# Cross-attention stages: ScalarE and VectorE in written order, norms in two pieces, the routing's norm behind a batch's second exponential

## The chip, the cores and the metric

One Trainium2 chip, of which one core is used. The time is the device time of one launch in microseconds (us), as the median of several runs. The engines are named as in the profile: PE (TensorE), DVE (VectorE), ACT (ScalarE), POOL (GpSimd) and SP (SyncE, which only issues transfers here). Each engine works through its own instruction stream in order and waits on semaphores for the others.

## The reference

Four layers act on `x` of shape (4, 512, 256) with a context `ctx` of shape (4, 64, 256). Each layer is an attention over the context, then a feed-forward part, both added to `x`.

```python
# layers 0 and 3: softmax attention, 16 heads of 16
q = _layernorm(x) @ Wq + bq;  k, v = ctx @ Wkv + bkv
x = x + softmax(q k^T / 4) v @ Wo + bo
# layer 1: the same over feature maps [exp(z), exp(-z)], z = heads @ fm_w^T + fm_b,
#          values of 32 per head, output through fc_w
# layer 2: a cosine alignment between x and ctx
# layers 0 and 3, feed-forward: 8 experts, 2 picked per token by a router
#          that works on _layernorm(x)
# layer 1: MLA self-attention, then a shared expert and 7 routed ones
# layer 2: a gated feed-forward with blockwise fp4 quantization
```

What matters here is a layer norm of every token, the projection to queries, scores against 64 keys per head, a largest score per head, an exponential, a sum and its reciprocal, the weighted values and the output projection; and in layers 0 and 3 a second layer norm of the result, router logits, the two best of eight experts and a table of where each token's row goes.

## The kernel before, in words

`x` stays in SBUF as 16 tiles of 128 tokens by 256 (`NT` = 16). Four tiles make one batch of the input (`GT` = 4, `B` = 4). The attention over the context of layers 0, 1 and 3 is one method, `xattn` (L637), called by `xattn_linear` for layers 0 and 3 and directly from `run` for layer 1. Below, L0, L1, L2 and L3 with no further number mean these layers; L followed by two or more digits is a line of the kernel.

**One batch's work** is divided into generators. `ctx_heads` (L618) is the front: layer norm of four tiles (`layernorm`, L326: per tile a `bn_stats` and a `bn_aggr` on DVE, one square root `ln_sd` on ACT, reciprocal `ln_rs` and shift `ln_sh` on DVE, then four Identity activations that write `xn`), the output bias added to `x` on POOL (L628), eight transposes (`ps_xT`) with copies to SBUF (`xnT`, in turn by ACT and DVE), the query projection (`ps_q`) and the batch's values (`ps_v`, `v`, `va`). `ctx_largest` (twice per batch, L516) computes scores `ps_cs` and their negative maxima `mx` (DVE); `ctx_turned` transposes these (`ps_mT`, `mT`). `ctx_weights` (twice per batch, L549) computes scores turned round in `ps_cx`, subtracts the maxima by four more products, and takes one exponential of 128 x 2048 (`cpr`, ACT, L563). There is a single PSUM buffer for `ps_cs` and `ps_cx` (`sc=1`, L642), so the next product there waits until its reader is done. `ctx_sums` sums the weights (`ps_den`) and takes the reciprocal `crs` (DVE, 128 x 512). `ctx_values` spreads `crs` over the head's columns (`ps_bc`, copied by ACT to `cbs`), multiplies with the weighted values (`ps_cy`, `cy` on DVE), and projects (`ps_p`, added to `x` on DVE).

**The routing** of a batch (`route`, L1143, in layers 0 and 3) has its own layer norm, eight transposes, router logits (`ps_r`, `r_lg`), the two best experts (`top2`, a chain of small DVE instructions), ranks by two small products (`ps_rank`), row addresses `e_at` (DVE), and eight indirect transfers of POOL that write the token rows to `xs` in DRAM (L859). From the second batch on a table of blocks is computed (DVE). SP then loads each expert block's tokens (`e_x`, L1008), which PE transposes (`ps_xe`, L1016) ahead of the block's large products (`ps_gu`). `begin` issues the first of these loads inside the last batch of `xattn`.

**The order.** A planner places instructions unless a region is entered with `in_order`, in which the engines named keep the order in which the Python code writes them. In `xattn` PE is in written order for the whole stage. In L1, where `before` is given, ACT, DVE and POOL are in written order too, for the first batch. The loop over batches interleaves three generators by hand with `some(gen, n)`, which advances a generator by n steps: `new`, the front of the next batch; `old`, `ctx_values` of the batch before, followed by its routing; and `late`, the rest of an older `old`. The list `soon` says how many steps of `new` go to each of five places. Behind a stage the expert blocks run in a region with DVE and SP in written order.

**Before L1** the results of L0's routed blocks are loaded from DRAM and added to `x` (`before.load`, `before.take`), on DVE for the first batch and on POOL for the others. L3 follows L2's feed-forward, whose fp4 steps (`f_y`, `f_c`, `f_am`) are on DVE and whose last product is `ps_fd` (L1655); L3's key copy `kT` (ACT, L427) and `kbd` (DVE, L399) come from the keys' product `ps_k`.

Of the kernel before, what the change touches and what calls it, by code (L numbers as in the profile page):

```python
# [14 lines left out]
PE, SP, ACT = mybir.EngineType.PE, mybir.EngineType.SP, mybir.EngineType.Activation  # L15
DVE, POOL = mybir.EngineType.DVE, mybir.EngineType.Pool
# [7 lines left out]
B, S, E = 4, 512, 256  # L24
# [3 lines left out]
GT = S // P  # L28
# [160 lines left out]
class Net:  # L189
# [425 lines left out]
                nc.vector.tensor_tensor(x, po[:, i], x, ALU.add)  # L615
            yield

    def ctx_heads(self, pool, st, query, values, bias, before):  # L618

        g = st.g  # L620
        if before:
            for i in range(GT):
                before.take(g * GT + i, self.nc.gpsimd if g else self.nc.vector)
        xn = self.xn_tile()
        self.layernorm(g, xn)
        for i in range(GT):
            x = self.x[g * GT + i]
            self.nc.gpsimd.tensor_tensor(x, x, self.row(bias), ALU.add)  # L628
        yield
        xT = self.transposed(xn)  # L630
        yield
        st.qs = query(pool, xT)
        yield
        st.va = values(pool, g)
        yield

    def xattn(self, query, values, scale, dv, W, bias, before=None, after=None, keys=None, begin=lambda: None):  # L637

        with self.room("xattn") as pool, self.banks(mm=4, sc=1), ExitStack() as stack:  # L642
            mxs = [pool.tile([P, 4, 32], F32, tag=f"mx{i}", name=f"mx{i}", bufs=1) for i in range(GT)]
            for m in mxs:
                self.nc.gpsimd.memset(m, 0.0)
            for t in range(NT if before else 0):
                before.load(pool, t, self.nc.scalar if t // GT == 1 else self.nc.sync, bufs=12)
            stack.enter_context(self.in_order(PE))
            if keys:
                for _ in self.ctx_ready(pool, keys):  # L650
                    pass
            sts = [SimpleNamespace(g=g, pr=[]) for g in range(B)]

            def heads(g):
                return self.ctx_heads(pool, sts[g], query, values, bias, before)

            def rest(st):
                yield from self.ctx_values(pool, st, dv, W)
                if after and st.g < B - 1:
                    yield from after(st.g)  # L660

            def some(gen, n=-1):
                while n and next(gen, self) is not self:
                    n -= 1

            nf = NH * dv // P
            old = late = iter(())
            new = heads(0)  # L670
            first = ExitStack()
            first.enter_context(self.in_order(ACT, DVE, POOL) if before else nullcontext())
            some(new)
            for st in sts:
                if st.g:
                    old = rest(sts[st.g - 1])
                new = heads(st.g + 1) if st.g + 1 < B else iter(())

                soon = [1, 0, 1, 1, 0] if st.g else [0, 0, 0, 1, 1]
                some(new, soon[0])  # L680
                self.ctx_largest(st, 0, mxs)
                some(old, 2)
                self.ctx_largest(st, 1, mxs)
                some(old, nf // 2)
                some(new, soon[1])
                self.ctx_turned(pool, st, mxs)
                some(new, soon[2])
                some(old, nf - nf // 2)
                some(late)
                if st.g == B - 1:  # L690
                    begin()
                self.ctx_weights(pool, st, 0, scale)
                some(new, soon[3])
                self.ctx_weights(pool, st, 1, scale)
                some(new, soon[4])
                some(old, 2)
                self.ctx_sums(pool, st)
                some(new)
                some(old, 2)
                late = old  # L700
                first.close()
            old = rest(sts[-1])
            for _ in old:
                some(late, 1)
            some(late)

# [90 lines left out]
class Routed:  # L799
# [282 lines left out]
    def begin(self, pool):  # L1082

        self.held, self.xb, self.wgu, self.wd = pool, {}, {}, {}

        self.weights(0, (True, False))
        for b in range(3):
            self.tokens(b)
        for b in range(1, 3):
            self.weights(b, (True, False))  # L1090
            self.tokens(b + 2)
# [41 lines left out]
    def take(self, t, eng):  # L1133

        x, r = self.net.x[t], self.loaded.pop(t)
        for k in range(2):
            eng.tensor_tensor(x, x, r[:, k], ALU.add)


class Layers(Net):  # L1140


    def route(self, moe, g, rw, fine=False):  # L1143


        def steps():
            rows = self.xn_rows()
            xn = rows[:, :, :E]
            yield from self.layernorm_steps(g, xn)
            moe.mark(g, rows)  # L1150
            yield True
            xT = self.transposed(xn)
            yield True
            lg = self.sm("r_lg", [P, GT, 8])
            self.nc.vector.tensor_copy(lg, self.scores(xT, rw, 8))
            yield True
            picked = self.top2(lg, 8, NEG, True, rows)
            yield True
            yield from moe.add(g, rows, *picked)
            yield True  # L1160

        return (whole for whole in steps() if whole or fine)
# [617 lines left out]
```

## Time and profile before

| | us |
|---|---|
| median of 3 runs | 1987.32 (1986.11 to 1991.52) |
| the profiled execution's own time | 1997.21 |
| its span | 1995.5 |
| PE busy | 1712.2 (86%) |
| DVE busy | 1020.4 (51%) |
| ACT busy | 671.4 (34%) |
| POOL busy | 424.3 (21%) |
| mean granted PE clock | 0.928 |

The three attention stages lie at about 0 to 165 us (L0), 535 to 704 us (L1) and 1560 to 1717 us (L3) of the span. PE is busy 119.1 of the first 165 us, 135.5 of the 169 us of L1's stage, and 123.7 of the 157 us of L3's.

In the profile, a line of the timeline gives start, duration, engine, line of code, operation, output and inputs, how many instructions it stands for, and in brackets the idle time of the engine just ahead of it with what ended that wait. A line of the waits gives what waited, for what, the total, how often and the longest. PEld is PE's loading of weights, which overlaps with its products.

### The profile page before, as it was taken

What the parts mean: (1) busy time and instruction counts of PE and PEld (TensorE: products, weight loads), DVE (VectorE), ACT (ScalarE), POOL (GpSimd) and SP (SyncE); (2) the same over time, 40 slices, a digit from 0 to 9 for tenths busy, and PEclk for the clock granted to TensorE, in tenths of its full rate; (3) what the DMA queues carried; (4) which work ended last, traced back from release to release, by engine and by line L of the source; (5) the groups of instructions that cost most, each with busy time, mean ns of one, the idle gap of its engine ahead of it and who ended that gap; (6) DMA issues with size and microseconds to landing.
All of it is one profiled execution on the core that took longest, in us unless ns stands there. A gap on an engine that the chain in (4) does not pass through costs nothing.

```text
span 1995.5 us, 25928 instructions
## 1 busy us (share of the span) xinstructions
PE 1712.2 (86%) x8752; PEld 970.5 (49%) x8752; DVE 1020.4 (51%) x3011; ACT 671.4 (34%) x1254; POOL 424.3 (21%) x594
## 2 busy tenths in 40 slices
PE   5878999999789868898989888985998887899993
PEld 2435666666444433343433344543665443455552
DVE  3655544444454343444454536546989565553333
ACT  3333222222254323335343432233445334222220
POOL 2031211111240021123131312223113103221112
PEclk8989999999899968998999999995899898999997
DMA  9528787887400100000001035972000001788884
GB/s 294 160 84 330 273 294 281 290 287 281 134 1 1 39 1 1 1 1 22 1 27 42 19 101 173 298 254 85 1 1 1 12 1 65 238 293 301 298 298 162
DMA packets 109350, 271.61 MB, mean 136 GB/s; under 512 B 13409, under 2 KB 71201, under 8 KB 99105
## 3 DMA queue, kind: packets, MB, share of 16 engines
q1 hardware_dynamic: 82976, 227.97, 33.9%
q0 software_dynamic: 10176, 28.00, 3.7%
q10 hardware_dynamic: 16064, 13.98, 2.1%
q8 instruction: 70, 1.15, 0.2%
q14 instruction: 64, 0.52, 0.1%
HBM read 220.48 MB, written 49.42 MB: 135 GB/s over the span
## 4 chain that ended last, share of the span: by engine, by line
PE 69%; DVE 18%; ACT 6%; issue 3%; DMA 2%; POOL 1%; SPq 0%; ACTq 0%; DVEq 0%; POOLq 0%
PE ps_gu L1030 20%; PE ps_de L1072 10%; PE ps_ms L1235 4%; PE ps_mo L1273 3%; DVE mq L1240 2%; PE ps_p L612 2%; PE ps_mx L1250 2%; PE ps_f L1633 2%; PE ps_xT L377 2%; PE ps_he L1059 2%; PE ps_bc L591 2%; ACT cpr L563 2%; PE ps_cx L557 1%; PE ps_ms L1238 1%; PE ps_cy L597 1%
## 5 line engine op out<-in xcount | busy, mean ns | idle before, releaser
L1030 PE MATMUL ps_gu<-e_wgu,e_xT 128*128 128x352 f32 (+1 forms) x1088 | 420.9, 526 | 13.1 <-DVE e_xT L1022 5.8
L1030 PEld LDWEIGHTS ps_gu<-e_wgu,e_xT 128*128 128x128 f32 x1088 | 195.5, 190 | 155.7 <-issue 71.4
L1072 PE MATMUL ps_de<-e_wd,e_hT 128*128 128x256 f32 x932 | 233.0, 387 | 10.8 <-ACT e_hT L303 3.1
L1075 POOL DMA_INDIRECT ys<-e_y,e_to x116 | 113.2, 976 | 482.6 <-ACT e_y L1074 336.5
L1072 PEld LDWEIGHTS ps_de<-e_wd,e_hT 128*128 128x128 f32 x932 | 172.8, 191 | 83.6 <-issue 39.0
L1047 DVE TENSOR_TENSOR e_h<-e_s,ps_gu 128x352 f32<-128x352 f32 (+2 forms) x155 | 83.4, 538 | 244.8 <-PE ps_gu L1030 185.0
L1240 DVE TENSOR_REDUCE mq<-ps_ms 128x2 f32<-128x256 f32 (+3 forms) x128 | 105.7, 826 | 139.9 <-PE ps_ms L1238 136.6
L1046 ACT ACTIVATE e_s<-ps_gu 128x352 f32<-128x352 f32 (+2 forms) x155 | 74.1, 478 | 280.3 <-PE ps_gu L1030 264.9
L1074 ACT ACTIVATE e_y<-ps_de,e_wt 128x256 f32<-128x256 f32 x116 | 55.0, 474 | 262.6 <-PE ps_de L1072 250.0
L1252 ACT ACTIVATE mpr<-ps_mx 128x1024 f32<-128x1024 f32 (+3 forms) x128 | 90.1, 704 | 146.9 <-PE ps_mx L1250 137.9
L1235 PE MATMUL ps_ms<-mkT,mqT 32*128 32x512 f32 (+3 forms) x512 | 111.7, 515 | 25.8 <-DVE mq L1240 24.3
L859 POOL DMA_INDIRECT xs<-xn,e_at x96 | 94.5, 985 | 120.4 <-DVE e_fi L893 39.7
L1250 PE MATMUL ps_mx<-mqm,mkT 32*128 32x128 f32 (+3 forms) x512 | 107.4, 497 | 1.3 <-ACT mpr L1252 1.3
L1254 POOL TENSOR_SCALAR_AFFINE_SELECT mpr<-mpr 128x256 f32<-128x256 f32 x128 | 52.2, 409 | 250.7 <-ACT mpr L1252 250.6
L1273 PE MATMUL ps_mo<-mpr,va 128*32 128x128 f32 (+3 forms) x512 | 97.1, 461 | 4.5 <-POOL mpr L1254 3.2
L1633 PE MATMUL ps_f<-w,xqT 128*128 128x352 f32 x256 | 86.1, 478 | 1.2 <-ACT xqT L1624 1.2
L1059 PE MATMUL ps_he<-consts_sb,e_h 128*128 128x128 f32 x466 | 76.3, 277 | 9.6 <-DVE e_h L1047 6.7
L557 PE MATMUL ps_cx<-q,kbd 32*128 32x512 f32 x256 | 45.2, 806 | 44.1 <-ACT cpr L563 44.1
L1235 PEld LDWEIGHTS ps_ms<-mkT,mqT 32*128 32x128 f32 x512 | 40.9, 195 | 80.6 <-DVE mq L1240 56.0
L1019 DVE COPY e_xT<-ps_xe 128x256 f32<-128x256 f32 x78 | 33.0, 423 | 86.7 <-PE ps_xe L1016 86.7
L377 PE MATMUL ps_xT<-consts_sb,xn 128*128 128x128 f32 x256 | 48.8, 330 | 32.4 <-ACT xn L345 18.7
L1059 PEld LDWEIGHTS ps_he<-consts_sb,e_h 128*128 128x128 f32 x466 | 53.7, 138 | 29.4 <-DVE e_h L1047 13.7
(317 smaller groups left out, 2816.0 us busy)
## 6 DMA issues: line engine op xcount, KB each, us to landing
e_wgu<-in_e0gu SPq DMA_DIRECT2D x39, 1408.0 KB
e_wgu<-in_e3gu SPq DMA_DIRECT2D x39, 1024.0 KB
e_wd<-in_e0d SPq DMA_DIRECT2D x39, 768.0 KB
e_wd<-in_e3d SPq DMA_DIRECT2D x39, 512.0 KB
e_wgu<-in_e1gu SPq DMA_DIRECT2D x38, 512.0 KB
xs<-z SPq DMA_DIRECT2D x16, 1040.0 KB
e_x<-xs SPq DMA_DIRECT2D x116, 130.0 KB
e_wd<-in_e1d SPq DMA_DIRECT2D x38, 256.0 KB
```

The source lines that it names most:

```text
L377: nc.tensor.transpose(ps[:, i * P : (i + 1) * P], x[:, i, c * P : (c + 1) * P], self.ident)
L859: r = nc.gpsimd.indirect_dma_start(out=net.xs, out_offset=bass.IndirectOffsetOnAxis(ap=at[:, k, i : i + 1], axis=0), in_=rows[:, i], in_of ...
L1030: nc.tensor.matmul(ps[:, :n], xT[:, c], wgu[:, c, cols], start=(c == 0), stop=(c == NC - 1))
L1059: self.nc.tensor.transpose(ps[:r, f - f0], h[:, f * P : f * P + r], net.ident)
L1072: nc.tensor.matmul(po[:, :E], hT[:r, f], wd[:r, f], start=(f == 0), stop=(f == self.nf - 1))
L1075: r = nc.gpsimd.indirect_dma_start(out=net.ys, out_offset=bass.IndirectOffsetOnAxis(ap=at, axis=0), in_=y, in_offset=None)
L1235: nc.tensor.matmul(ps[:, r, :n], st.qT[o][rows, diag], st.kT[o][rows, :n], start=True, stop=False)
L1240: nc.vector.tensor_reduce(st.q[:, i, at : at + 2, HD], ps[:, :, :n], AX.X, ALU.max, negate=True)
L1250: nc.tensor.matmul(ps[:, r, :n], st.kT[o][rows, keys], st.qm[o][rows, j * P :], start=True, stop=True)
L1252: nc.scalar.activation(pr[:, :, :n], ps[:, :, :n], AF.Exp, scale=HD**-0.5)
L1273: nc.tensor.matmul(st.po[32 * n : 32 * n + 32, j * P :], st.va[:, j, at : at + 32], pr[:, r, : S - j * P], start=(j == 0), stop=(j == GT - 1),
L1633: nc.tensor.matmul(ps[:, :H], xT[:, c], w[:, c, k * H : (k + 1) * H], start=(c == 0), stop=(c == NC - 1))
```

## The change

In `xattn`, ACT and DVE join PE in written order for the whole stage, and L1's special region for its first batch goes. The transfers' results (`take`) are no longer added inside `ctx_heads` but by a small function that is called for batches 0 and 1 at the start and for batch g + 2 in iteration g. `ctx_heads` runs its layer norm in two steps: statistics and square root in the first; reciprocal, Identity and the bias in the second. `route` likewise gives back control after its norm's first half. `soon` has four places, and the places of the generators in the loop are other ones: in batches 1 to 3 one step of `new` (the next norm's statistics) comes ahead of the first `ctx_largest`, its second half behind it; one step of `late` (routing) follows; two steps of `old`'s routing norm come behind the second `ctx_weights`. In batch 0 three steps of `new` (norm and transposes) stand between the two `ctx_weights`. Behind the loop the last batch's values and the remaining routing are interleaved one to one.

```diff
-    def ctx_heads(self, pool, st, query, values, bias, before):
+    def ctx_heads(self, pool, st, query, values, bias):
 
         g = st.g
-        if before:
-            for i in range(GT):
-                before.take(g * GT + i, self.nc.gpsimd if g else self.nc.vector)
         xn = self.xn_tile()
-        self.layernorm(g, xn)
+        yield from self.layernorm_steps(g, xn)
...
-            stack.enter_context(self.in_order(PE))
+            stack.enter_context(self.in_order(PE, ACT, DVE))
+
+            def take(g):
+                for t in range(g * GT, (g + 1) * GT if before and g < B else 0):
+                    before.take(t, self.nc.gpsimd if g else self.nc.vector)
+
+            take(0)
+            take(1)
...
-            old = late = iter(())
+            old = iter(())
             new = heads(0)
-            first = ExitStack()
-            first.enter_context(self.in_order(ACT, DVE, POOL) if before else nullcontext())
             some(new)
             for st in sts:
+                late = old
                 if st.g:
                     old = rest(sts[st.g - 1])
                 new = heads(st.g + 1) if st.g + 1 < B else iter(())
-
-                soon = [1, 0, 1, 1, 0] if st.g else [0, 0, 0, 1, 1]
+                take(st.g + 2)
+
+                soon = [1, 1, 1, 1] if st.g else [0, 0, 0, 3]
                 some(new, soon[0])
                 self.ctx_largest(st, 0, mxs)
+                some(new, soon[1])
+                some(late, 1)
                 some(old, 2)
                 self.ctx_largest(st, 1, mxs)
                 some(old, nf // 2)
-                some(new, soon[1])
                 self.ctx_turned(pool, st, mxs)
                 some(new, soon[2])
                 some(old, nf - nf // 2)
...
                 self.ctx_weights(pool, st, 0, scale)
                 some(new, soon[3])
                 self.ctx_weights(pool, st, 1, scale)
-                some(new, soon[4])
                 some(old, 2)
+                if not st.g:
+                    some(new, 1)
                 self.ctx_sums(pool, st)
                 some(new)
                 some(old, 2)
-                late = old
-                first.close()
-            old = rest(sts[-1])
-            for _ in old:
-                some(late, 1)
-            some(late)
+            last = rest(sts[-1])
+            for _ in last:
+                some(old, 1)
+            some(old)
...
-            yield from self.layernorm_steps(g, xn)
+            for _ in self.layernorm_steps(g, xn):
+                yield True
             moe.mark(g, rows)
             yield True
```

More of the change, by code (lines that the diff above doesn't have):

```diff
@@ L654, in heads @@
             def heads(g):
-                return self.ctx_heads(pool, sts[g], query, values, bias, before)
+                return self.ctx_heads(pool, sts[g], query, values, bias)
             def rest(st):
```

## The prediction

> **What bounds the kernel now.** I read the page's busy shares, then the waits of TensorE, then the timeline of single iterations. Page, parts 1 and 5 (engine, busy, share; group, then busy and mean ns, then idle time ahead of it and what ended it):
>
> ```profile
> PE 1712.2 (86%) x8752; PEld 970.5 (49%) x8752; DVE 1020.4 (51%) x3011; ACT 671.4 (34%) x1254; POOL 424.3 (21%) x594
> ...
> L557 PE MATMUL ps_cx<-q,kbd 32*128 32x512 f32 x256 | 45.2, 806 | 44.1 <-ACT cpr L563 44.1
> ```
>
> TensorE is the bound, above all in the expert blocks, which the change does not touch; a delay of the attention stages passes on to the end through them. Inside the three attention stages TensorE waits, and 44.1 us of that is for an exponential to free the single score bank. By stage (waits of TensorE in the first 170 us, then 1560 to 1720: what waited, on what, total us, times, longest):
>
> ```profile
> PE ps_cx L557 <- ACT cpr L563: 19.3, 4, 8.4
> ```
> ```profile
> PE ps_cx L557 <- ACT cpr L563: 19.1, 4, 8.3
> ```
>
> So 38.4 us in L0 and L3 together, 5.7 in L1. Why ScalarE is late shows in the timeline of L0's second batch (start, duration):
>
> ```profile
> 59.43 0.33 PE L545 MATMUL ps_mT<-consts_sb,mx 128*128 128x128 f32 x1 [0.23 <-DVE mx L534]
> ...
> 60.89 1.28 ACT L339 ACT_TABLE_LOAD   x1
> ...
> 65.93 0.30 ACT L339 ACTIVATE ln_sd<-ln_mv,eps 128x4 f32<-128x4 f32 x1 [1.51 <-DVE ln_rs L342]
> ...
> 66.14 3.54 ACT L345 ACTIVATE xn<-x,ln_sh,ln_rs 128x256 f32<-128x256 f32 x7
> ...
> 69.70 1.28 ACT L563 ACT_TABLE_LOAD   x1
> 70.99 1.88 ACT L563 ACTIVATE cpr<-ps_cx 128x2048 f32<-128x2048 f32 x1
> ...
> 72.92 1.23 PE L557 MATMUL ps_cx<-q,kbd 32*128 32x512 f32 x4 [5.00 <-ACT cpr L563]
> ```
>
> The scores are ready at 64.3, but both norms (the next batch's and the routing's) sit on ScalarE ahead of the exponential, 11.6 us after the last maximum (M, 59.4).
>
> **The change, part by part.** I place each instruction of the new written order with the durations above. Batches are 0 to 3; shifts in us, plus is later.
>
> *Batch 0 (L0, L3).* The next norm is put between the two exponentials: table load 1.28, ln_sd 0.30, reciprocal and shift 0.5, four Identity 2.07, and TensorE has the transposes ahead of ps_cx(1), so it sits idle and ps_cx then costs 2.09 + 1.93 (row at 139.23) instead of 1.14 + 1.04. exp0 to exp1 is 11.05 instead of 4.0 (39.15 to 43.15) in L0, and instead of 5.8 in L3 (1588.00 to 1593.79): +7.05 and +5.3; the reciprocal crs (3.36) then ends 0.75 behind what q covered in L0. **+7.8, +5.3.** The Trainium skill (ScalarE: Activation LUTs, Table sets: the hidden batching unit and What ACT_TABLE_LOAD costs) speaks against this: exps go together, since a switch costs 1.28 and a drain of 1.38. The row 69.70 has exp start 0.01 after a load of 1.28, with no drain; so two loads are 2.56 by row, 5.3 by rule, which would add 2.8 to each stage. I take the row.
>
> *Batch 1.* VectorE in written order has four pairs of statistics of the next batch (0.42 + 0.18, pitch 0.54: 2.2) ahead of the first maximum; VectorE was free to take mx at once: +2.0. Gain: ahead of exp0 ScalarE has only mT copy 0.59 and a table load that lies beside ps_cx; TensorE's mT 0.5, transposes 1.04, p 1.9, ps_cx 2.2 set exp0 at M + 5.4 instead of M + 11.6: −6.2. q (3.7) covers exp0, so ps_cx(1) no longer waits. Loss: the routing's norm stands behind exp1 (1.88): load 1.28, ln_sd 0.30; VectorE's rs/sh at +4.0, and crs 3.36 follows these, then v, va 0.84, xnT 0.69, and r's 16 matmuls 1.85: 10.8 from exp1 to r's end where it was 5.6 (76.78 to 82.45), and the next ps_cs stands behind r on TensorE: +5.2. **+1.0.**
>
> *Batch 2.* Statistics +1.1 (part in VectorE's slack). ps_rank now stands ahead of ps_cx(0) and needs VectorE's chain of top2 and masks (0.2 each, 17 links), so exp0 gains only 2.85. Routing norm +4.5. **+2.75.**
>
> *Batch 3 and the end.* Batch 1's routed rows are written to DRAM by eight indirect DMAs of POOL, and the first block's tokens e_x are loaded by SP behind them (timeline):
>
> ```profile
> 130.83 1.04 POOL L859 DMA_INDIRECT xs<-xn,e_at  x1 [19.93 <-DVE e_fi L893]
> ...
> 144.60 2.00 SPq L1008 DMA_DIRECT2D e_x<-xs  x3
> ...
> 148.71 0.78 PE L1016 MATMUL ps_xe<-consts_sb,e_x 128*128 128x128 f32 x4
> ...
> 150.47 1.12 PE L591 MATMUL ps_bc<-crs,pairs_sb 128*128 128x512 f32 x2 [0.97 <-DVE r_lg L1155]
> ```
>
> With M at 126.2: scatters begin M + 4.6, take 8 × 1.27 = 10.2, ps_xe runs at M + 22.5, in step with the rest. In the new order e_at comes behind four x on VectorE, so scatters begin M + 6.7 and e_x lands about M + 24.6, while TensorE has ps_xe **ahead** of the routing's transposes and is there at M + 15. It stands for 9 to 10 us; behind it are ps_xe 0.78, transposes 1.97 (cold), copy 0.7, r 1.95, so ps_bc comes at M + 30 instead of M + 24.3: +5.7. What batch 3 saves before (3.7 at exp0) is swallowed here. Last, VectorE's top2, table and cy run in one line; from ps_bc to the first ps_gu it was 14.8; the wait of top2 for the first cy adds between 1 and 4.7, I take +3. The M shift takes −0.5. **+8.2.**
>
> L0: 7.8 + 1.0 + 2.75 + 8.2 = **+19.7** (its start is bound by Wkv's load and the copy ahead of q as before, 0). L3 the same with 5.3: **+17.2.**
>
> *L1* (no routing): exp1 +2.5 and ps_bc −0.3 in batch 0, statistics ahead of maxima +1.75 in batch 1 and +3.6 in batch 2 (three of the next layer's ride along), a load less −0.5. **+7.0**, between +3 (VectorE slack) and +9. The hoisted adds lie on POOL, which is 21% busy: 0.
>
> *L3's start.* Before, three of L3's norms, the transposes and most of q ran inside L2's tail. There the key copy waited for L2's last product:
>
> ```profile
>   PE ps_fd L1655: 2.9, 1
> ```
>
> (the copy kT's one line of idle time: ended by ps_fd, 2.9 us, once.) With ScalarE and VectorE in written order, the first norm follows kbd, which follows kT, so all is exposed after ps_fd's end F: x and kT 0.9, kbd 1.1, statistics 2.2, ln_sd and rs 0.8, xn 2.07, last transpose 0.5, copy 0.7, q 6.61 (cold, as in L0 at 19.95), its copy 0.6: ps_cs at F + 15.5. F was 1573.95; L2's tail sheds twelve pairs (7 us) of a VectorE that is 19.9 of 20 us busy (1520 to 1540) and 2.8 us of q from TensorE: F earlier by 2.8 to 7, take 4.5. ps_cs at 1585 instead of 1575.97: **+9**, from +6.5 to +10.7. The skill's clock rule (TensorE: Matmul & The Clock Gate, What's actually happening) gives half clock for the first 3.4 us of work only, so q 4.4, 2.2 less; L0's row has 0.50 granted after 5 us of work (22 to 25). I keep the row.
>
> **Sum.** 19.7 + 7.0 + 9 + 17.2 = +52.9. On the profiled execution's 1997.2 (span 1995.5) that is 2050; it lies 9.9 over the median, and since waits grow, not matmuls, I carry the difference over whole: 1987.3 + 52.9 = **2040**.
>
> **Rivals.** *Milder:* the scatters are no later than before, or TensorE's written order lets ps_xe cost nothing, and L2's tail shrinks by as much as L3's start grows: −17.4 (5.7 + 3, twice) − 9: +26.5, 2014. For it: POOL still goes by the scheduler, VectorE is the bound in L2's tail. Against: eight scatters at 1.27 are one queue, and ps_xe stands first on TensorE.
>
> *Faster:* the exponentials no longer behind two norms. Place: ps_cx's wait in batches 1 to 3; price: all of 38.4 plus six warm ps_cx (4.0 to 2.1, 11.4) = 49.8 gained, of which my sum counts only 18.1 because other late things eat it. Batch 0 (13.1) and L3's start (9) stay: −27.7, 1960. It decides if the other costs (statistics ahead of mx, routing norm behind exp1, ps_xe, the end: 21 a stage, 7 in L1, 49 in all) come to less than 27.7. For it: VectorE 51%, ScalarE 34% busy. Against: r and ps_cs stand on TensorE behind just this norm.
>
> *No effect:* both balance, or the scheduler's order is as good as written: 1987.
>
> **How the numbers follow.** Full sum 0.55 (own range 2022 to 2062), milder 0.25, faster 0.12, no difference 0.03 (within 0.3%, what a measurement can tell), worse than 2062 0.05 (drain by rule, VectorE chain longer). The range takes in the milder case and stops just above the old time at 1990; up to 2065. Faster 0.12, same 0.03, slower 0.85.
>
> **What would show it.** Right: ps_cx's wait for cpr goes from 44 to under 20; 11 us between batch 0's two exponentials; TensorE idle about 9 us ahead of ps_xe in L0 and L3; ps_cs of L3 some 15 us behind ps_fd; no L3 norm inside L2. Wrong: r ending 6 us behind exp1, ps_xe without a wait, or L2 ending over 7 us earlier.

## The result and the profile after

The changed kernel takes 2060.36 us (2055.98 to 2062.15, 4 runs) where the kernel before takes 1986.71 us: a ratio of 1.0367, with a 95% interval of 1.0338 to 1.0396. It is 74 us slower, in the forecast direction and inside the range, 5 us below its upper end of 2065; the likeliest value, 2040, was 20 us too low.

The first profile of before belonged to an execution of 1997 us, 10 over its median. A second profile of the same kernel (an experiment below, 1986.02 us, span 1984.3) is the better base for the profile after (span 2059.0). By stage, from landmarks on TensorE:

| stretch | before (second profile) | after | difference | predicted |
|---|---|---|---|---|
| L0 up to the first ps_gu | 167.3 | 192.2 | +24.8 | +19.7 |
| first ps_gu to the first ps_ms (blocks, then L1's attention) | 570.3 | 573.6 | +3.3 | +7.0 |
| ps_ms to the last ps_mo (self-attention) | 423.2 | 427.6 | +4.4 | 0 |
| last ps_mo to ps_fd's end F (blocks, L2) | 404.8 | 404.0 | −0.8 | −4.5 |
| F to L3's first ps_cs | 2.0 | 14.8 | +12.8 | +13.5 |
| L3's first ps_cs to its first ps_gu | 139.2 | 167.0 | +27.8 | +17.2 |
| first ps_gu to the end | 277.5 | 279.9 | +2.4 | 0 |
| sum | 1984.3 | 2059.0 | +74.7 | +52.9 |

TensorE's busy time is 1706.7 us in the second profile of before and 1744.9 us after, for the same 8752 products: 38.2 of the 74.7 us are products that ran longer, and only the rest is idle time. TensorE in L0 up to the first ps_gu (stretch, its length, busy time with the number of products, granted clock, DMA share and GB/s), before in the second profile, then after:

```profile
0.00:167.34 167.34, 121.26 (x789) 0.86 0.66 188
```
```profile
0.00:192.15 192.15, 134.84 (x789) 0.81 0.59 177
```

So L0's +24.8 is 13.6 us of longer products and 11.2 of idle time. In L3, from its first scores to its first ps_gu, it is 16.0 (107.2 to 123.2 us busy) and 11.8, and the granted clock goes from 0.87 to 0.80. That the added waits lowered the clock fits, but no run separates the two.

The waits of TensorE in the first 190 us of the kernel after (what waited, on what, total us, times, longest):

```profile
PE ps_xT L377 <- ACT xn L345: 11.5, 10, 4.7
PE ps_xe L1021 <- DMA e_x<-xs: 8.8, 1, 8.8
...
PE ps_rank L849 <- DVE e_pm L844: 5.3, 3, 3.1
PE ps_p L612 <- DVE cy L605: 4.2, 3, 2.4
```

The wait of ps_cx for the exponential, 19.3 us before, is down to 2.0; the change does what it says. Over the whole kernel it is 7.1 of 44.1 (the group of ps_cx among the groups of after, same columns as in the prediction):

```profile
L557 PE MATMUL ps_cx<-q,kbd 32*128 32x512 f32 x256 | 43.6, 781 | 7.2 <-ACT cpr L563 7.1
```

Four waits grew in its place: for norms, for the tokens e_x, for the ranks, and for the products cy. They come to 29.8 us; in the second profile of before they took 3.6, 0.8, 1.5 and 1.3, together 7.2.

The timeline of L0's batch 1 (start, duration, then what), before (first profile, ahead of the rows in the prediction) and after the change:

```profile
46.21 3.36 DVE L581 RECIPROCAL crs<-ps_den 128x512 f32<-128x512 f32 x1 [1.30 <-PE ps_den L572]
...
50.57 1.17 PE L526 MATMUL ps_cs<-kbd,q 32*128 32x128 f32 x32
51.81 2.36 DVE L534 TENSOR_REDUCE mx<-ps_cs 128x16 f32<-128x1024 f32 x2 [0.25 <-PE ps_cs L526]
...
57.02 2.36 DVE L534 TENSOR_REDUCE mx<-ps_cs 128x16 f32<-128x1024 f32 x2 [0.34 <-PE ps_cs L526]
```
```profile
54.90 3.36 DVE L581 RECIPROCAL crs<-ps_den 128x512 f32<-128x512 f32 x1 [8.88 <-PE ps_den L572]
...
61.05 2.32 DVE L534 TENSOR_REDUCE mx<-ps_cs 128x16 f32<-128x1024 f32 x2
61.21 1.28 ACT L339 ACT_TABLE_LOAD   x1 [7.50 <-DVE ln_mv L337]
...
63.74 2.07 ACT L345 ACTIVATE xn<-x,ln_sh,ln_rs 128x256 f32<-128x256 f32 x4 [0.93 <-ACT ln_sd L339]
...
65.72 1.04 ACT L593 COPY cbs<-ps_bc 128x512 f32<-128x512 f32 x2
66.31 1.29 DVE L605 TENSOR_TENSOR cy<-ps_cy,cbs 128x512 f32<-128x512 f32 x2 [2.66 <-ACT cbs L593]
...
67.52 2.34 DVE L534 TENSOR_REDUCE mx<-ps_cs 128x16 f32<-128x1024 f32 x2
```

The second scores were done at 64.7, yet their maxima start at 67.5: VectorE has cy ahead of them, cy needs the copies cbs, and cbs stands on ScalarE behind the next batch's whole norm, which stands behind its statistics. From first scores (55.8) to last maximum (69.9) it is 14.0 us where it was 8.8. From there to the exponential it is 5.7 where it was 11.6. What the exponential gained, the maxima lost. The first maxima are late as well: they start 5.2 us behind the first scores, where it was 1.2. Of that, 2.1 us are the norm's statistics (58.92 to 61.05). The rest is the reciprocal crs with v and va behind it: crs ended 1.0 us ahead of the first scores and now ends 2.4 behind them, as batch 0's sums of weights now stand behind the query on TensorE. Batch 2 has one more link, the routing's small exponential t_e on ScalarE, again ahead of cbs:

```profile
101.10 0.20 ACT L756 ACTIVATE t_e<-t_d 128x4 f32<-128x4 f32 x1 [0.69 <-DVE t_d L755]
101.21 1.05 ACT L593 COPY cbs<-ps_bc 128x512 f32<-128x512 f32 x2
101.81 1.29 DVE L605 TENSOR_TENSOR cy<-ps_cy,cbs 128x512 f32<-128x512 f32 x2 [0.75 <-ACT cbs L593]
...
103.01 2.35 DVE L534 TENSOR_REDUCE mx<-ps_cs 128x16 f32<-128x1024 f32 x2
```

The routing's norm behind the second exponential (81.17 in batch 1), and what is behind it on TensorE:

```profile
83.07 1.28 ACT L339 ACT_TABLE_LOAD   x1
...
85.16 2.07 ACT L345 ACTIVATE xn<-x,ln_sh,ln_rs 128x256 f32<-128x256 f32 x4 [0.50 <-DVE ln_sh L343]
...
89.73 2.34 PE L738 MATMUL ps_r<-router_w_sb,xnT 128*128 128x8 f32 x14 [1.05 <-DVE xnT L305]
92.00 2.09 PE L526 MATMUL ps_cs<-kbd,q 32*128 32x128 f32 x32
```

From the second exponential to the next scores it is 10.83 us; it was 5.67. L0's end after the change, then L3's start behind L2's last product, in the second profile of before and after (TensorE, same view):

```profile
165.32 1.44 PE L1021 MATMUL ps_xe<-consts_sb,e_x 128*128 128x128 f32 x4 [8.79 <-DMA e_x<-xs]
```
```profile
1562.70 2.95 PE L1655 MATMUL ps_fd<-w,hqT 128*128 128x256 f32 x12
...
1567.67 1.41 PE L526 MATMUL ps_cs<-kbd,q 32*128 32x128 f32 x32
```
```profile
1592.77 4.52 PE L1661 MATMUL ps_fd<-w,hqT 128*128 128x256 f32 x12
1602.93 2.80 PE L377 MATMUL ps_xT<-consts_sb,xn 128*128 128x128 f32 x8 [5.64 <-ACT xn L345]
1605.66 5.64 PE L498 MATMUL ps_q<-xnT,w_qT_sb 128*128 128x512 f32 x8
1612.10 1.17 PE L526 MATMUL ps_cs<-kbd,q 32*128 32x128 f32 x32
```

TensorE stands 8.8 us for e_x, and L3's norm, transposes and query all lie open behind L2.

### The profile page after: what moved, and what is told of

It reads as the page before. It is cut to its first block, busy times and chain, and to the rows that moved or that the text cites. A ratio compares the mean times of both kernels' runs of the same rounds, so it can differ in the third digit from the quotient of the medians.

```text
span 2059.0 us, 25940 instructions
## 1 busy us (share of the span) xinstructions
PE 1744.9 (85%) x8752; PEld 992.6 (48%) x8752; DVE 1032.0 (50%) x3011; ACT 678.8 (33%) x1258; POOL 422.7 (21%) x594
## 4 chain that ended last, share of the span: by engine, by line
PE 68%; DVE 18%; ACT 5%; issue 3%; POOL 2%; DMA 2%; ACTq 0%; SPq 0%; DVEq 0%; POOLq 0%
PE ps_gu L1035 20%; PE ps_de L1077 9%; PE ps_ms L1241 4%; PE ps_mo L1279 3%; PE ps_f L1639 2%; PE ps_p L612 2%; DVE mq L1246 2%; PE ps_xT L377 2%; DVE mx L534 2%; PE ps_mx L1256 2%; PE ps_q L498 2%; PE ps_fd L1661 2%; DVE crs L581 2%; PE ps_cx L557 2%; POOL xs L864 2%
## 5 line engine op out<-in xcount | busy, mean ns | idle before, releaser
L1035 PE MATMUL ps_gu<-e_wgu,e_xT 128*128 128x352 f32 (+1 forms) x1088 | 426.8, 532 | 20.0 <-DVE e_xT L1024 9.5
L1077 PE MATMUL ps_de<-e_wd,e_hT 128*128 128x256 f32 x932 | 231.5, 385 | 10.9 <-ACT e_hT L303 5.1
L377 PE MATMUL ps_xT<-consts_sb,xn 128*128 128x128 f32 x256 | 57.0, 348 | 60.2 <-ACT xn L345 46.2
L625 POOL TENSOR_TENSOR x<-x,rows_sb 128x256 f32<-128x256 f32 x48 | 33.7, 731 | 220.8 <-ACT xn L345 157.4
L377 PEld LDWEIGHTS ps_xT<-consts_sb,xn 128*128 128x128 f32 x256 | 37.1, 170 | 82.7 <-ACT xn L345 61.5
```

The lines of the kernel that those rows point to most:

```text
L377: nc.tensor.transpose(ps[:, i * P : (i + 1) * P], x[:, i, c * P : (c + 1) * P], self.ident)
L1035: nc.tensor.matmul(ps[:, :n], xT[:, c], wgu[:, c, cols], start=(c == 0), stop=(c == NC - 1))
L1077: nc.tensor.matmul(po[:, :E], hT[:r, f], wd[:r, f], start=(f == 0), stop=(f == self.nf - 1))
```

## The experiments

My theory was that the written order of ScalarE and VectorE is the cost: what stands behind a waiting instruction there waits along. The first rival was that the new places cost and the order is harmless; others stand with each run. They are counted in the order in which they stand. A ratio is to the kernel before, measured beside the run: 1989.40 us for the first four, 1989.65 for the fifth to the eighth, 1993.38 for the last four runs. A comparison with the changed kernel is one of medians, or of ratios where the base differed.

**Order without the new places.** The kernel before with one edit:

```diff
-            stack.enter_context(self.in_order(PE))
+            stack.enter_context(self.in_order(PE, ACT, DVE))
```

> The kernel before with one word of the change: ScalarE and VectorE join TensorE in written order, all places and norms as before. Theory (the written order itself costs): the code before already writes batch 0's next norm between the two exponentials and the routing's norm behind the second one, and only the planner had moved them forward, so most of the loss is here: 40 to 90 us slower than before, 11 us between batch 0's exponentials, L3's first scores 12 to 16 us behind ps_fd. Rival (the new places cost, the order is harmless): within 10 us of before.

Measured: 2059.33 us, ratio 1.0356 (1.0332 to 1.0380), the same as the changed kernel within the intervals. L3's first scores came 14.8 us behind ps_fd. Batch 0's exponentials were 7.3 us apart, not 11. So the written order alone, with the old places, costs as much as the whole change; the new places repair nothing of it on balance.

**New places without the order.** The changed kernel with `in_order(PE)` only.

> The changed kernel with only TensorE in written order, ScalarE and VectorE left to the planner. Theory: the planner moves norms forward again, exponentials 4 to 6 us apart in batch 0, L3's norms back inside L2's tail; within 10 us of before, either way. Rival (the new places cost): 30 to 75 us slower than before, ps_xe still waits 6 to 9 us.

Measured: 2025.66 us, ratio 1.0190 (1.0173 to 1.0207), some 36 us slower than before and 35 faster than the changed kernel. Both expectations missed in part. Batch 0's exponentials were 4.0 us apart in L0, L3's first scores 2.0 behind ps_fd, and ps_xe came at 152.5 with 0.7 us of waits, as the theory had it; but the places have a cost of their own. Against the second profile of before it lies at +5.7 in L0, +14.0 in L3 from first scores to first ps_gu, and +10.4 between L0's first ps_gu and ps_ms. In L0 and L3 the routing's transposes and logits stand behind the second exponential's sums on TensorE here too: from that exponential to the next scores it is 9.0 to 10.9 us in batches 1 and 2, where the second profile of before has 5.7 to 6.6. For L1 the diff offers a cause that no run tests alone: with this edit nothing puts L1's first batch in order any more, and its first exponential came 422 us behind L0's first ps_gu where before and after have 401. The costs of places and order are not a sum: order alone +70, places alone +36, both +74.

**Written order from behind the first front on.** Two lines in the changed kernel:

```diff
-            stack.enter_context(self.in_order(PE, ACT, DVE))
+            stack.enter_context(self.in_order(PE))
...
             some(new)
+            stack.enter_context(self.in_order(ACT, DVE))
             for st in sts:
```

> The changed kernel, but ScalarE and VectorE enter the written order only behind the stage's first front (keys, first norm, query). Theory (L3's start is exposed by the order): L3's first scores come 1 to 4 us behind ps_fd instead of 14.8, and the time falls by 8 to 13 us against the changed kernel. Rival (L2's tail takes it all back, as it is bound by VectorE): falls by less than 4 us.

Measured: 2044.79 us, ratio 1.0279 (1.0260 to 1.0297), 15.6 us less than the changed kernel and more than the 8 to 13 expected, as L0 starts earlier too. TensorE at L3's start in this run:

```profile
1589.36 2.95 PE L1662 MATMUL ps_fd<-w,hqT 128*128 128x256 f32 x12
1592.24 1.98 PE L498 MATMUL ps_q<-xnT,w_qT_sb 128*128 128x512 f32 x4
...
1595.02 1.17 PE L526 MATMUL ps_cs<-kbd,q 32*128 32x128 f32 x32
```

Four of the query's eight matmuls are back inside L2's tail (only four are left behind ps_fd), and the scores follow ps_fd by 2.7 us instead of 14.8. L0's first scores come at 19.4, which I had not expected: the changed kernel has them at 25.2, where the first norm stands behind kbd, and the kernel before at 27.4, where the planner had put another batch's statistics ahead of the first norm's reciprocal (before, VectorE):

```profile
12.36 0.43 DVE L336 BATCH_NORM_STATS2 ln_st<-x 128x6 f32<-128x256 f32 x1 [2.84 <-DMA x<-in_x]
```

These wait for x of a later batch, and the reciprocal follows at 12.93; in this run it starts at 9.42. The rival fell: from the last ps_mo to ps_fd's end it is 403.6 us in this run and 404.0 in the changed kernel, so L2's tail takes nothing back. But only L3's first norm is inside L2 here, four of the twelve pairs of statistics that the kernel before has there.

**Batch 0's norm ahead of its exponentials.**

```diff
-                soon = [1, 1, 1, 1] if st.g else [0, 0, 0, 3]
+                soon = [1, 1, 1, 1] if st.g else [1, 1, 0, 1]
```

> The changed kernel, but in batch 0 both halves of the next norm stand around the first maxima instead of between the two exponentials (transposes stay between). Theory: the gap between batch 0's exponentials falls from 11.2 (L0) and 10.5 us (L3) to 5 to 6, the maxima come up to 2.5 later; 6 to 12 us less than the changed kernel over the three stages. Rival (the gap only moves, what bounds is VectorE's maxima): less than 3 us.

Measured: 2048.08 us, ratio 1.0299 (1.0282 to 1.0317), 12.3 us less. ScalarE in L0's batch 0:

```profile
39.42 1.88 ACT L563 ACTIVATE cpr<-ps_cx 128x2048 f32<-128x2048 f32 x1 [1.87 <-PE ps_cx L561]
...
43.42 1.88 ACT L563 ACTIVATE cpr<-ps_cx 128x2048 f32<-128x2048 f32 x1 [1.64 <-PE ps_cx L561]
```

The exponentials are 4.0 us apart in L0 and L3, 4.8 in L1 (11.3 after). First scores to the first ps_gu fell by 4.3 us in L0 and 3.8 in L3. The two profiles are 10.0 us apart, and another 2.3 of these lie between the last ps_mo and ps_fd's end, a stretch that this edit doesn't touch. In L1 the gap's 6.5 us bought nothing: from L0's first ps_gu to ps_ms it is 573.8 against 573.6, since the first exponential came 7 us later.

**The norm behind cbs and cy.**

```diff
-                some(new, soon[0])
                 self.ctx_largest(st, 0, mxs)
-                some(new, soon[1])
                 some(late, 1)
                 some(old, 2)
+                some(new, soon[0])
+                some(new, soon[1])
                 self.ctx_largest(st, 1, mxs)
```

> The changed kernel, but in batches 1 to 3 both halves of the next norm stand behind the first maxima, the copies cbs and the products cy, ahead of the second maxima. Theory (in the changed order cbs and cy stand behind the norm on ScalarE and VectorE, which is what lengthened first scores to last maximum from 8.8 to 14.0 us in L0's batch 1 and from 10.4 to 13.4 in batch 2): it falls to 10 to 11.5 in batch 1; 3 us in each of six batches, 8 to 18 us less than the changed kernel. Rival (VectorE's sum of work is the same, only its sequence changes): less than 4 us.

Measured: 2060.44 us, ratio 1.0360 (1.0337 to 1.0382): no gain, the rival held. cbs and cy did come early (cy ends at 64.2 in batch 1), but first scores to last maximum stayed at 14.0 us. The first maxima still start 3.1 us behind the scores, with no statistics ahead of them, as crs, v and va are; then:

```profile
66.39 1.28 ACT L339 ACT_TABLE_LOAD   x1 [3.42 <-DVE ln_mv L337]
...
68.02 0.18 DVE L342 RECIPROCAL ln_rs<-ln_sd 128x4 f32<-128x4 f32 x1 [1.70 <-ACT ln_sd L339]
...
68.31 2.35 DVE L534 TENSOR_REDUCE mx<-ps_cs 128x16 f32<-128x1024 f32 x2
```

Now VectorE's maxima stand behind the reciprocal, that behind the square root, and that behind a table load that waited for the statistics: VectorE idles 1.70 us, with 2.2 of statistics ahead of it. The norm's round trip between the two engines has to lie somewhere in one line of instructions.

**The routing's norm between the exponentials.**

```diff
                 self.ctx_weights(pool, st, 0, scale)
+                some(old, 2)
                 some(new, soon[3])
                 self.ctx_weights(pool, st, 1, scale)
-                some(old, 2)
```

> The changed kernel, but the routing's norm stands between a batch's two exponentials instead of behind both. Theory (behind the second one it delays the logits, and with them the next batch's scores on TensorE): second exponential to next first scores falls from 10.8 and 11.6 us to 6 to 8, the exponentials move 1 to 3 us apart; ps_xT of the last routing goes ahead of ps_xe; 8 to 20 us less than the changed kernel. Rival (the norm costs the same wherever it stands): within 5 us of the changed kernel.

Measured: 2061.89 us, ratio 1.0369 (1.0339 to 1.0399): the rival held. In batch 1 the exponentials moved 3.0 us apart (8.5 for 5.6), as expected, but from the second to the next scores it is still 9.5 (10.8 without this edit), not 6 to 8. TensorE's waits in this run, first 200 us:

```profile
PE ps_den L572 <- ACT cpr L563: 13.9, 3, 6.0
```

TensorE has the sums of the weights ahead of the routing's transposes, and these sums wait for the later exponential. In L0 the transposes did go ahead of ps_xe, and ps_xe to the first ps_gu took 23.7 us instead of 26.8; the later exponentials took it back.

**The routing's norm ahead in the last batch alone.** The same `some(old, 2)` ahead of the first `ctx_weights`, in batch 3 only.

> The changed kernel, but in the last batch alone the routing's norm stands ahead of the first exponential. Theory (TensorE waits 8.8 and 6.2 us for e_x ahead of ps_xe in L0 and L3, so a later exponential there is free, and the transposes and logits that stood behind ps_xe come first): the exponentials come 3 to 5 us later, ps_bc comes 2 to 5 us earlier, 4 to 10 us less than the changed kernel over both stages. Rival (VectorE's chain of top2 and table is what ends last there): less than 2 us.

Measured: 2069.70 us, ratio 1.0412 (1.0391 to 1.0433), 9 us slower than the changed kernel. The theory fell. The exponential came not 3 to 5 but 12 us later (29.9 behind the batch's first scores, 17.6 in the changed kernel), since the square root found its statistics not done:

```profile
154.75 0.30 ACT L339 ACTIVATE ln_sd<-ln_mv,eps 128x4 f32<-128x4 f32 x1 [12.18 <-DVE ln_mv L337]
```

The slack ahead of ps_xe was smaller than the delay put into it.

**Before, once more**, with a profile.

> The kernel before, unchanged, a second profile of it. In the changed kernel and in four others the stretch from the first ps_ms to the last ps_mo of layer 1's self-attention takes 427.6 to 428.5 us, in the first profile of before 435.3, whose execution was 10 us over the median. If that execution was slow there, it is 427 to 429 here and the sum of stages has to be set against this profile; if the change did it, 435 again.

Measured: 1986.02 us; the self-attention took 423.2 us, less than the 427 to 429 expected. So the first profile of before had lost 12 us there by an execution, not by a difference of the kernels. In the other kernels this stretch takes 423 to 438 us; the 4.4 us that the changed kernel shows there are within that spread, and I leave them open.

**One engine in order at a time.** `in_order(PE, ACT)` and `in_order(PE, DVE)` in the changed kernel.

> The changed kernel with TensorE and ScalarE in written order, VectorE left to the planner. With neither (places alone) it was 36 us slower than before, with both 71 to 74. Theory (what stands behind a waiting instruction on ScalarE, the copies cbs behind ln_sd and t_e, and L3's first norm behind kT, is the larger part of the order's cost): 2045 to 2060. Rival (VectorE's order is: the maxima behind statistics, top2 and cy): 2022 to 2035.

> The changed kernel with TensorE and VectorE in written order, ScalarE left to the planner. Theory (ScalarE's order is the larger part): 2025 to 2042. Rival (VectorE's is): 2045 to 2062; L3's first scores 14 us behind ps_fd in that case, since kbd then heads VectorE's line.

Measured: ratio 1.0287 (1.0264 to 1.0309) for ScalarE and 1.0305 (1.0281 to 1.0329) for VectorE; the chip's base was 1993.4. Neither is the larger part, the intervals overlap: each alone adds some 20 us to the 1.0190 of the places, both together 35. The two added up would give 1.0402, both together gave 1.0367; the difference is within the intervals, so whether they overlap isn't shown. With VectorE alone L3's scores come 14.8 behind ps_fd, with ScalarE alone 12.1, so either line is enough to hold L3's first norm back.

**top2 behind the second maxima.**

```diff
-                some(late, 1)
                 some(old, 2)
                 self.ctx_largest(st, 1, mxs)
...
                 self.ctx_turned(pool, st, mxs)
+                some(late, 1)
                 some(new, soon[2])
```

> The changed kernel, but the routing's top2 (VectorE, 12 small instructions, and t_e on ScalarE) stands behind the second maxima and their transposes instead of ahead of cbs and cy. Theory (t_e waits for top2 on ScalarE with cbs behind it, cy and the second maxima behind that on VectorE): first scores to second scores' last maximum in batch 2 falls from 13.4 to 9 to 11 us, in batch 3 from 11.2 to 9 to 10, of which the later ps_rank takes at most half back: 4 to 12 us less than the changed kernel over four batches. Rival (the chain only moves to ahead of ps_rank and ps_cx): within 3 us.

Measured: 2067.85 us, ratio 1.0362 (1.0341 to 1.0383), no gain. In L0 first scores to last maximum fell from 13.4 to 11.7 us in batch 2, not to 9 to 11, and in batch 3 it is 11.3 as before the edit (11.2). First scores to first exponential fell from 21.5 to 19.3 us in batch 2 and rose from 17.6 to 20.8 in batch 3, as ps_rank and with it ps_cx now stand behind the chain. The rival held.

**Three places mended at once**: the edits of written order behind the first front, batch 0's norm, and top2.

> The changed kernel with three places mended: written order only behind the first front, batch 0's norm ahead of its exponentials, top2 behind the second maxima. If the costs add: 15.5 (measured for the first) plus 12.3 (for the second) plus what top2 gives, 2020 to 2033, still 30 to 45 us slower than before. If they overlap: 2038 or more. Below 1987 it would beat both kernels, which neither theory expects.

Measured: ratio 1.0213 (1.0194 to 1.0231), 2034.91 us beside 1993.38. That is 0.0154 below the changed kernel, 31 us; the first two edits alone gave 0.0088 and 0.0068, which add to 0.0156. Within the intervals the first two gains add up, with nothing left over for top2's place. No version beat the kernel before; with ScalarE and VectorE in written order this is the nearest. What the runs point to, and what was not tried, is the kernel before with only L0's first batch taken from here: the next batch's first scores come at 46.5 us in this run and at 50.6 in the first profile of before, an estimate of 4 us to be had. All of it lies ahead of L0's own first scores (23.4 and 27.4).

## Why the prediction was right, and where it was short

By its own steps, on the batches of L0 (first profile of before, as the prediction used it):

| step | predicted | measured |
|---|---|---|
| batch 0, exponential to exponential | 11.05 us | 11.18 (L0), 10.5 (L3) |
| batch 0, second exponential to ps_bc | +0.75 | +0.76 |
| batch 1, statistics ahead of the maxima | +2.0 | +5.2 |
| batch 1, last maximum to exponential | 5.4 us (its four parts add to 5.6) | 5.7 |
| batch 1, second exponential to next scores | 10.8 us | 10.83 |
| batch 2, same three | +1.1, −2.85, +4.5 | +3.0, −2.7, +5.3 |
| batch 3, statistics | −0.5 | +0.9 |
| batch 3, last maximum to ps_bc | 30 us | 29.8 |
| ps_xe's wait | 9 to 10 us | 8.8 (L0), 6.2 (L3) |
| last ps_bc part to the first ps_gu | +3 (1 to 4.7) | +5.1 |
| L3's first scores behind ps_fd | 15.5 us | 14.8 |
| L2's tail shorter | 2.8 to 7, taken 4.5 | 3.1 (see below) |
| L1 | +7.0 (3 to 9) | +3.3 |

The mechanism was the forecast one: the wait for the exponential went, and what waits on ScalarE and VectorE in one line took more than it gave. About half of the terms came out within half a microsecond. Two had been weighed against the Trainium skill. The table load cost its row of 1.28, with no drain as in "ScalarE: Activation LUTs" (What ACT_TABLE_LOAD costs): 11.18 us between batch 0's exponentials, not 13.8. For the query behind L2's end the row had 6.61, and 4.4 was the estimate from the 3.4 us of half clock in "TensorE: Matmul & The Clock Gate" (What's actually happening); it took 5.64, between the two. From 1602.90 to 1609.60 TensorE was busy for 6.61 of 6.70 us, and the granted clock was 0.50 throughout.

What was short above all is one term: *statistics of the next batch ahead of the first maximum, +2.0 and +1.1*. It measured +5.2 and +3.0. The statistics themselves took their 2.1 us; the term counted nothing else. In the timeline above crs, v and va are ahead of batch 1's first maxima too, and then the rest of that norm, from batch 2 on with t_e, stands ahead of cbs on ScalarE, cy waits for cbs, and the second maxima stand behind cy on VectorE (2.8 us behind their scores in batch 1). I had asked what is queued behind the norm's VectorE part, and not behind its ScalarE part. Experiment five shows that putting cbs first doesn't win it back, as the table load and the square root then stand ahead of the maxima instead.

L0 and L3 hold most of the 21.8 us between sum and measurement. In L3, against the second profile, the shift grew by 4.3 us in batch 0, 6.7 in batch 1, 6.4 in batch 2 and 10.4 in batch 3 with the end, where I had 5.3, 1.0, 2.75 and 8.2: 10.6 too little. In L0 it was 5.9, 3.9, 5.7 and 11.1 where I had 7.8, 1.0, 2.75 and 8.2, less 1.7 at the start: 5.1 too little. The self-attention (4.4) and the blocks behind L3 (2.4) were not forecast, the stretch that ends with L2 gave 0.8 instead of 4.5, and L1 was 3.7 too high. So 2040 came as near as it did in part by luck, as terms that were too high met terms that were too low. And "waits grow, not matmuls" did not hold: half of the growth is in the products' own time, and the sum counted longer products only in places, such as batch 0's ps_cx and L3's query. L0's start was not bound as I had put it, by Wkv and a copy: in experiment three its first scores come 8 us before the old time, with the keys' product at 8.7 us (8.8 before).

The end was longer for a like reason: VectorE waits 3.67 us for the first cy with top2 behind it, t_e waits for top2 with the second cbs behind it, and the ranks wait 3.05 us.

L2's tail did give time back, but hardly for the reason that I gave, VectorE busy 19.9 of 20 us with twelve pairs of statistics. From the 65th of L2's 256 ps_f products to ps_fd's end it is 151.2 us in the first profile of before, 151.6 in the second and 151.2 with the places alone, all with three of L3's norms inside L2; after the change, with none, it is 148.1. (The stretch from the last ps_mo shows only 0.8 of this, as what lies ahead of the tail took 2.7 us longer in that execution; from layer 1's last ps_gu to L2's first ps_f alone it is 45.5 us, and 42.5 to 45.8 in the others.) But with ScalarE alone in order ten of the twelve pairs are still inside L2, without their Identity activations, and the tail takes 148.0. So the pairs there did not cost the time; what of the three norms did stays open. Busy time of an engine in a window is not time on its critical path.

The faster rival is refuted by a direct reading: the waits of ps_cx for the exponential did go (37 of 44.1 us over the whole kernel, 34.4 of the 38.4 in L0 and L3 that it counted), and larger ones took their place. The milder one had ps_xe for nothing, and ps_xe waits 15.0 us in both stages together.

## What to carry to other kernels

A written order on an engine makes each of its instructions wait for all that stand ahead, so each place has to be checked on every engine that the placed step uses: for a norm here VectorE, ScalarE and VectorE again, with a table load in between. When a planner's order leaves a visible stall, write down what it had moved forward elsewhere before taking the order from it; here that was norms inside the layer before and between batches, worth more than the 38 us of stalls. The idle time that an order adds to an engine need not be the whole price: here TensorE's products ran longer as well. Work that leaves a busy engine gives time back only if it stood on the path.

## What the runs showed of the hardware that was not expected

A table load does not always run while its engine idles: in batch 1 ScalarE was idle for 7.50 us and the load started only when the statistics it served were done (61.21), so its 1.28 us lay on the path; in experiment seven the load of the same line ran at 141.29, 13 us ahead of its square root. The half clock at L3's start lasted 6.7 us of nearly unbroken work on TensorE (1602.90 to 1609.60, granted 0.50).
